# Reciprocal softmax sums for the values' product: float16 halves through DMA transposes instead of float32 transposes on TensorE

## The chip, the core and the metric

One core of a Trainium2 chip runs one launch. The metric is device time in microseconds (us) from start to end of that launch, less being better. The engines are PE (TensorE, matrix products), DVE (VectorE), ACT (ScalarE), POOL (GpSimd) and SP (SyncE, which here only issues DMAs); each takes its instructions in the order in which the program lists them and waits on semaphores for the others.

## What is computed

A transformer block on x of 16 batches, 512 tokens, 512 channels, in float32: one normalised input feeds a causal 16-head attention and a gated feed-forward layer, and both are added to x.

```python
xn = _layernorm(x, axis=-1)
x = x + _L0_attn_ref(xn, w_qkv, b_qkv, w_out, b_out) + _L0_ffn_ref(xn, gate_w, up_w, down_w, gate_s, up_s, down_s)
# attention: 16 heads of 32 channels
scores = jnp.einsum('bhqd,bhkd->bhqk', q, k) / math.sqrt(Hd) + causal[None, None]
attn = jax.nn.softmax(scores, axis=-1)
out = jnp.einsum('bhqk,bhkd->bhqd', attn, v)
# feed-forward: 1408 inner channels
hdn = jax.nn.silu(g) * u
```

The kernel does the softmax without dividing: it makes exp(score - row maximum), multiplies these by the values, and divides the product by the row sums. What the change is about is how the reciprocals of the row sums reach the place where that division is made. The sums lie one query per partition, as 16 columns (4 query blocks x 4 heads); the product of a group of four heads lies the other way, 4 heads x 32 channels on the partitions and 512 queries along the row. So each reciprocal has to be repeated over 32 channels and transposed.

## The kernel before, in words

Weights stay in SBUF. All float32 operands of products are split in two 16-bit halves, a high one and the rest, so that a product is three matmuls with 16-bit operands (two for the feed-forward layer, whose weights are small integers).

The program is not written in the order in which it runs. It is a list of steps, each with an engine, an assumed duration, the buffers that it reads and writes, and, for PE, a key: the time at which it should run. `Plan.order` (line 98) simulates the five engines with these durations, picks for PE the ready step of lowest key and for the others the one that is ready first (`slack` shifts that), and hands out the numbered buffers as it goes. The order it finds is the order of the instructions on every engine, fixed at build time. If the chip takes other times than the assumed ones, an engine waits at the instruction whose input is late, and everything listed behind it on that engine waits too.

The work is cut into 64 slots, one for each of 16 batches and 4 groups of four heads (loop at line 916). A slot holds

- the scores of its own group, in three pieces (`soft_run`, line 505): query block 3, block 2, blocks 1 and 0. Behind each piece come row maxima on DVE (L556), exponentials on ACT, which also sum the rows into `den` (L561), the split of the exponentials into two halves `pq` on ACT (L581) and DVE (L586), and a DMA transpose `pT<-pq` for each query block, issued by SP (L595);
- the values' product `av` of the group of the slot before (`av_step`, line 601), at 7 us (`AV_LAG`) into the slot by its key;
- fillers: the q and k projections of the next group (`qk_proj`), some of the 11 feed-forward chunks of the batch (`ffn_chunk`), the v projections of the batch in the first slot (`v_proj`), the output projection of the batch before in the second, the down projection in the fourth.

In `av_step` the reciprocals travel so: DVE takes them (`rden`, L615), POOL spreads each over 32 columns as float32 (`rb`, L618), PE transposes four 128x128 squares into a PSUM bank (`R`, L628), ACT copies that to SBUF (`Rs`, L631), DVE multiplies the product by it (L654), and ACT and POOL split the result in halves `oh` and `ol` (L655, L656) for the output projection.

Buffers that matter here: the tag `mm`, three PSUM banks, through which all projections, the feed-forward products and `R` go; the tag `tmp32`, four buffers of 512 float32, for the q, k projection (`qkt`), the v projection (`vt`), the feed-forward chunk (`ft`) and `rb`; the tag `r32`, one such buffer, for `Rs`; one PSUM bank for `av`.

Of the kernel before, what the change touches and what calls it, by code (L numbers as in the profile page):

```python
# [9 lines left out]
F16 = mybir.dt.float16  # L10
# [4 lines left out]
ALU = mybir.AluOpType  # L15
# [6 lines left out]
P = 128  # L22
# [3 lines left out]
NG = H // 4  # L26
# [3 lines left out]
def newton_rsqrt(nc, y, v, t):  # L30

    yi = y.bitcast(I32)
    nc.vector.tensor_scalar(yi, v.bitcast(I32), 1, None, ALU.logical_shift_right)
    nc.vector.tensor_scalar(yi, yi, -1, 0x5F3759DF, ALU.mult, ALU.add)
    for _ in range(3):
        nc.vector.scalar_tensor_tensor(t, v, -0.5, y, ALU.mult, ALU.mult)
        nc.vector.tensor_tensor(t, t, y, ALU.mult)
        nc.vector.scalar_tensor_tensor(y, t, 1.5, y, ALU.add, ALU.mult)


class Tile:
# [21 lines left out]
class Plan:  # L63
# [34 lines left out]
    def order(self):  # L98
        for n, st in enumerate(self.steps):
            st.n, st.left = n, len(st.deps)  # L100
            for d in st.deps:
                d.next.append(st)
        free = dict.fromkeys(self.ENGINES, 0.0)
        ready = {e: [] for e in self.ENGINES}
        made, done, dma = {}, [], 0.0

        def begin(st):
# [12 lines left out]
            return t  # L120

        def release(st):
            st.at = max([d.end - d.lat * (d.eng == st.eng != "SP") for d in st.deps], default=0.0)
            ready[st.eng].append(st)

        for st in self.steps:
            if not st.left:
                release(st)
        while len(done) < len(self.steps):
            best = None  # L130
            for e in self.ENGINES:
# [32 lines left out]
def fast_path(ctx, tc, good, x, wqkvT, bqk, bv, woT, bo, wgT, wuT, wdT, gs, us, dsc, out):  # L164
# [3 lines left out]
    nc = tc.nc  # L168
# [50 lines left out]
    wd = cp.tile([P, IC, D], F8, name="wd")  # L219

    st = [dict() for _ in range(NB)]
    grp = {}
    NSLOT = NB * NG
    MM4 = 0.864

# [14 lines left out]
                step.key = t  # L240
                t += dur * k

    def mm_group(f, ps, ops, piece=4, first=0, n=None):


        n = len(ops) if n is None else n

        def run(k0, k1):
            for k in range(k0, k1):
                l, r = ops[k][0]()  # L250
                nc.tensor.matmul(ps(), l, r, start=(first + k == 0), stop=(first + k == n - 1))  # L251

        prev = []
# [189 lines left out]
    def qk_proj(f, b, g, which):  # L443
        s = st[b]
        off = which * 512 + g * P
        nm = f"{b}_{g}_{which}"
        ps, t = mm("qk_" + nm), tmp32("qkt_" + nm)
# [17 lines left out]
            r=[ps, "bqk"], w=[t], slack=-3,  # L465
# [4 lines left out]
            r=[t, h], w=[l] + (["first"] if b == 0 and g == 0 else []), slack=-3,  # L470
# [3 lines left out]
    def v_proj(f, b, tb):  # L474
        s = st[b]
        ps, t = mm(f"v_{b}_{tb}"), tmp32(f"vt_{b}_{tb}")
        if tb == 0:
# [27 lines left out]
    def soft_run(b, g, blocks):  # L505
# [31 lines left out]
        def exps(i):  # L537
# [2 lines left out]
        both = lambda t: [(t, i) for i in blocks]  # L540
        run = add(
            "PE", 0.3 + 3 * cols / 2400.0, scores, r=[qh, ql, kh, kl],
            w=[tok for t in pss for tok in both(t)] + ([f"slot{b * NG + g}"] if blocks[0] == 3 else []),
            lat=0.3,
        )
        for u, i in enumerate(blocks):
# [27 lines left out]
        for i in blocks:  # L574
# [21 lines left out]
                r=[(pq, i, 0), (pq, i, 1)], w=[("pT", i)], lat=0.19 * 8 * (i + 1), slack=-5,  # L596
            )
            base += 8 * n
        return run

    def av_step(b, g):
# [6 lines left out]
        rb = work("rb_" + nm, "tmp32", 4)  # L608
# [7 lines left out]
        add(  # L616
            "POOL", gps(512),
            lambda: nc.gpsimd.tensor_scalar(  # L618
                rb().rearrange("p (c d) -> p c d", d=32),
                rden().unsqueeze(2).to_broadcast([P, 16, 32]),  # L620
                2.0 ** -15, None, ALU.mult,
            ),
            r=[rden], w=[rb],
        )

        def spread():
            for i in range(4):
                nc.tensor.transpose(R()[:, i * P : (i + 1) * P], rb()[:, i * P : (i + 1) * P], ident)  # L628

        first = add("PE", 0.5, spread, r=[rb], w=[R], lat=0.3)  # L630
        add("ACT", act(512), lambda: nc.scalar.copy(r(), R()), r=[R], w=[r], slack=-3)  # L631

        def run():
            for side, k0 in ((0, 0), (1, 0), (0, 1), (1, 1), (0, 2), (0, 3)):
# [12 lines left out]
                            skip_group_check=True,  # L647
                        )

        second = add(  # L650
            "PE", 2.3, run, r=[("pT", i) for i in range(4)] + [(t, tb) for t in (vh, vl) for tb in range(NT)],
            w=[av], lat=0.3,
        )
        add("DVE", dve(512), lambda: nc.vector.tensor_tensor(r(), av(), r(), ALU.mult), r=[av, r], w=[r], slack=-2)  # L654
        add("ACT", act(512), lambda: nc.scalar.copy(oh(), r()), r=[r], w=[oh], slack=3)  # L655
        add("POOL", gps(512), lambda: nc.gpsimd.tensor_tensor(ol(), r(), oh(), ALU.subtract), r=[r, oh], w=[ol])  # L656
        return first, second


    def ffn_chunk(f, b, ic):  # L660
# [129 lines left out]
        )  # L790

    def count_good(when, key):
        ps, ps1, limits = mm("flagT"), mm("flagR"), tmp32("limits")
# [40 lines left out]

    def attention_slot(s):

        av, runs = (), []
        if s > 0:
            av = av_step(*divmod(s - 1, NG))
        if s < NSLOT:  # L840
            b, g = divmod(s, NG)
            grp[(b, g)] = dict(den=work(f"den_{b}_{g}", "den", 2, (P, 16)))
            runs = [(soft_run(b, g, bl), sum((i + 1) * P + 250 for i in bl)) for bl in ((3,), (2,), (1, 0))]

        def place(t0, T):
            for k, step in enumerate(av):
                step.key = t0 + AV_LAG + (k - 1) * 1.5
# [301 lines left out]
```

## Time and profile before

| What | Value |
|---|---|
| time, median of 3 runs (lowest to highest) | 1915.01 us (1914.96 to 1915.26) |
| profiled execution, whole | 1915.52 us |
| its span, first to last instruction | 1913.7 us |
| mean granted clock of TensorE | 0.997 |
| SP's queue: 256 DMA transposes pT<-pq | 5.5 us from issue to landing, median |
| DMA packets of the hardware queue | 65.7% of 16 engines' span |
| chip memory traffic over the span | 38 GB/s |

How to read the page that the prediction quotes. A group line says: line, engine, operation, output<-inputs, shape, count, then busy time in us, mean ns of one, then the idle time of the engine just before such instructions and who ended it. The busy time of PE is the union of modelled durations of pipelined matmuls; what a matmul costs PE when it is kept fed is the distance from its start to the start of the next one, read from the timeline. A DMA row's time runs from issue to landing. A window row gives, for each engine, how many us of that window it was busy, and at its end the granted clock (1.00 is full) and the share of the 16 DMA engines in use.

### The profile page before, as it was taken

What the parts mean: (1) busy time and instruction counts of PE and PEld (TensorE: products, weight loads), DVE (VectorE), ACT (ScalarE), POOL (GpSimd) and SP (SyncE); (2) the same over time, 40 slices, a digit from 0 to 9 for tenths busy, and PEclk for the clock granted to TensorE, in tenths of its full rate; (3) what the DMA queues carried; (4) which work ended last, traced back from release to release, by engine and by line L of the source; (5) the groups of instructions that cost most, each with busy time, mean ns of one, the idle gap of its engine ahead of it and who ended that gap; (6) DMA issues with size and microseconds to landing.
All of it is one profiled execution on the core that took longest, in us unless ns stands there. A gap on an engine that the chain in (4) does not pass through costs nothing. (4 is left out here: it accounts for less than half of the span.)

```text
span 1913.7 us, 40913 instructions
## 1 busy us (share of the span) xinstructions
PE 1877.3 (98%) x15250; PEld 892.2 (47%) x15250; DVE 1482.0 (77%) x3541; ACT 1335.2 (70%) x3185; POOL 983.5 (51%) x713
## 2 busy tenths in 40 slices
PE   7899999999999999999999999999999999999997
PEld 3344444444444444444444444444444444444443
DVE  7778778797887978878788787877869787686674
ACT  5766757677676776767767676776767767677673
POOL 4446455464554646456464554645546454564533
PEclk9999999999999999999999999999999999999999
DMA  9875757666676656767567586667766667666465
GB/s 169 144 127 120 133 128 154 129 130 121 132 153 128 145 109 138 143 135 144 110 133 144 122 148 123 139 121 140 153 127 135 119 136 148 127 130 106 97 118 115
DMA packets 769519, 252.39 MB, mean 132 GB/s; under 512 B 734368, under 2 KB 738848, under 8 KB 769312
## 3 DMA queue, kind: packets, MB, share of 16 engines
q1 hardware_dynamic: 764688, 247.54, 65.7%
q0 software_dynamic: 4624, 2.16, 1.4%
q8 instruction: 121, 1.98, 0.4%
q14 instruction: 86, 0.70, 0.1%
HBM read 55.85 MB, written 16.78 MB: 38 GB/s over the span
## 5 line engine op out<-in xcount | busy, mean ns | idle before, releaser
L561 ACT ACTIVATE p<-s,negm 128x512 f32<-128x512 f32 (+3 forms) x1024 | 529.0, 531 | 231.3 <-DVE negm L556 229.1
L586 DVE SCALAR_TENSOR_TENSOR pq<-p,pq 128x2048 f16<-128x2048 f32 (+3 forms) x256 | 425.7, 1676 | 238.5 <-ACT pq L581 229.2
L556 DVE CUSTOM_DVE_ANT_0 s<-s,mask 128x512 f32<-128x512 f32 (+3 forms) x1024 | 473.1, 517 | 53.0 <-PE s L527 45.2
L581 ACT ACTIVATE pq<-p 128x2048 f16<-128x2048 f32 (+3 forms) x256 | 324.0, 1291 | 10.3 <-DMA pT<-pq 8.4
L691 POOL TENSOR_TENSOR hl<-ft,hh 128x512 f16<-128x512 f32 x176 | 226.9, 1295 | 190.1 <-ACT hh L690 189.3
L469 POOL TENSOR_TENSOR qkl<-qkt,qkh 128x512 f16<-128x512 f32 x128 | 165.1, 1290 | 244.7 <-ACT qkh L467 233.9
L251 PE MATMUL g<-xh,wg 128*128 128x512 f16 x704 | 267.6, 380 | 4.3 <-ACT qkt L464 2.4
L251 PE MATMUL u<-xh,wu 128*128 128x512 f16 x704 | 266.9, 379 | 2.8 <-DVE ft L681 1.5
L251 PE MATMUL dn<-wd,hh 128*128 128x512 fp8e4 x704 | 268.2, 381 | 0.0
L251 PE MATMUL dn<-wd,hl 128*128 128x512 fp8e4 x704 | 267.4, 380 | 0.0
L251 PE MATMUL g<-xl,wg 128*128 128x512 f16 x704 | 266.9, 379 | 0.0
L251 PE MATMUL u<-xl,wu 128*128 128x512 f16 x704 | 266.8, 379 | 0.0
L690 ACT CAST hh<-ft 128x512 f16<-128x512 f32 x176 | 109.3, 622 | 170.5 <-DVE ft L687 170.3
L618 POOL TENSOR_SCALAR rb<-rden 128x512 f32<-128x512 f32 x64 | 137.7, 2151 | 175.9 <-DVE rden L615 175.9
L251 PEld LDWEIGHTS <-wu 128*128 128x128 fp8e4 x1408 | 137.1, 98 | 169.7 <-issue 5.6
L561 ACT ACTIVATION_READ_ACCUMULATOR p<-s,negm 128x1 f32 x1024 | 214.5, 209 | 0.0
L251 PEld LDWEIGHTS <-wg 128*128 128x128 fp8e4 x1408 | 132.6, 98 | 159.6 <-issue 10.3
L251 PEld LDWEIGHTS <-wq_h 128*128 128x128 f16 x1024 | 95.4, 98 | 133.8 <-issue 28.5
L677 ACT ACTIVATE ft<-g,gt_c 128x512 f32<-128x512 f32 x176 | 121.1, 688 | 43.7 <-PE g L251 43.1
L407 POOL TENSOR_TENSOR xnl<-xc,xnh 128x512 f16<-128x512 f32 x60 | 96.7, 1612 | 104.5 <-DMA xl<-xnl 58.4
L687 DVE SCALAR_TENSOR_TENSOR ft<-u,gu_c,ft 128x512 f32<-128x512 f32 x176 | 132.0, 750 | 21.4 <-PE u L251 5.5
L717 POOL TENSOR_TENSOR xr<-xr,bo_b 128x512 f32<-128x512 f32 x64 | 94.4, 1475 | 103.9 <-DMA xr<-in_x 103.9
(114 smaller groups left out, 3205.3 us busy)
## 6 DMA issues: line engine op xcount, KB each, us to landing
xc<-in_x SPq DMA_DIRECT2D x64, 256.0 KB, 4.0
xr<-in_x SPq DMA_DIRECT2D x64, 256.0 KB, 2.9
out<-y SPq DMA_DIRECT2D x64, 256.0 KB, 2.5
pT<-pq SPq DMA_TRANSPOSE x256, 5.5
wq<-in_wqkvT SPq DMA_DIRECT2D x12, 256.0 KB, 5.4
exact<-in_wdT SPq DMA_DIRECT2D x11, 256.0 KB, 2.9
exact<-in_wgT SPq DMA_DIRECT2D x8, 256.0 KB, 3.0
exact<-in_wuT SPq DMA_DIRECT2D x8, 256.0 KB, 2.9
```

Source lines behind the costliest of these rows:

```text
L251: nc.tensor.matmul(ps(), l, r, start=(first + k == 0), stop=(first + k == n - 1))
L407: add("POOL", gps(512), lambda: nc.gpsimd.tensor_tensor(l(), xc(), h(), ALU.subtract), r=[xc, h], w=[l], slack=2)
L469: "POOL", gps(512), lambda: nc.gpsimd.tensor_tensor(l(), t(), h(), ALU.subtract),
L556: nc.vector.tensor_tensor_reduce(sc, sc, mask[:, 512 - n :], -(2.0 ** -7), 3e38, ALU.add, ALU.min, negm()[:, m : m + 1])
L561: nc.scalar.activation(exps(i).rearrange("p (k j) q -> p k j q", j=4)[:, :, j, :], part().rearrange("p (k q) -> p k q", q=P), AF.Exp, bias ...
L581: "ACT", act(4 * n), lambda src=src, half=half: nc.scalar.mul(half(0), src(), 2.0 ** 15),
L586: lambda src=src, half=half: nc.vector.scalar_tensor_tensor(half(1), src(), 2.0 ** 15, half(0), ALU.mult, ALU.subtract),
L618: lambda: nc.gpsimd.tensor_scalar(rb().rearrange("p (c d) -> p c d", d=32), rden().unsqueeze(2).to_broadcast([P, 16, 32]), 2.0 ** -15, Non ...
L677: "ACT", act(512) + 0.1, lambda: nc.scalar.activation(t(), pg(), AF.Tanh, scale=gt_c[:, ic : ic + 1]),
L687: lambda: nc.vector.scalar_tensor_tensor(t(), pu(), gu_c[:, ic : ic + 1], t(), ALU.mult, ALU.mult),
L690: add("ACT", act(512), lambda: nc.scalar.copy(hh(), t()), r=[t], w=[hh], slack=3)
L691: add("POOL", gps(512), lambda: nc.gpsimd.tensor_tensor(hl(), t(), hh(), ALU.subtract), r=[t, hh], w=[hl])
```

## The change

The reciprocals no longer go through PE. DVE takes `rden` as before and makes two float16 halves of it, scaled by 2^12; POOL spreads both halves over 32 columns (1024 float16 columns in place of 512 float32); SP issues a DMA transpose of that into an SBUF buffer `R`; POOL adds the two halves into the float32 factor `r`; DVE's multiplication takes the scale back. The four PE transposes and ACT's copy are gone.

```diff
-        R = mm("R_" + nm)
-        r = work("Rs_" + nm, "r32", 1)
+        rh = work("rh_" + nm, "rh", 2, (P, 2, 16), F16)
+        rb = work("rb_" + nm, "tmp32", 4, (P, 1024), F16)
+        R = work("R_" + nm, "r32", 1, (P, 8, P), F16)
+        r = tmp32("Rs_" + nm)
...
-        add("DVE", 0.15, lambda: nc.vector.reciprocal(rden(), d["den"]()), r=dens, w=[rden], slack=2)
+        def halves():
+            nc.vector.reciprocal(rden(), d["den"]())
+            nc.vector.tensor_scalar(rh()[:, 0, :], rden(), 2.0 ** 12, None, ALU.mult)
+            nc.vector.scalar_tensor_tensor(rh()[:, 1, :], rden(), 2.0 ** 12, rh()[:, 0, :], ALU.mult, ALU.subtract)
+
+        add("DVE", 0.6, halves, r=dens, w=[rden, rh], slack=2)
+        add(
+            "POOL", gps(1024),
+            lambda: nc.gpsimd.tensor_copy(
+                rb().rearrange("p (c d) -> p c d", d=32),
+                rh().rearrange("p z c -> p (z c)").unsqueeze(2).to_broadcast([P, 32, 32]),
+            ),
+            r=[rh], w=[rb],
+        )
+        add("SP", 1.3, lambda: nc.sync.dma_start_transpose(R(), rb()), r=[rb], w=[R], lat=1.5)
         add(
             "POOL", gps(512),
-            lambda: nc.gpsimd.tensor_scalar(
-                rb().rearrange("p (c d) -> p c d", d=32),
-                rden().unsqueeze(2).to_broadcast([P, 16, 32]),
-                2.0 ** -15, None, ALU.mult,
+            lambda: nc.gpsimd.tensor_tensor(
+                r(), R()[:, 0:4, :].rearrange("p i q -> p (i q)"), R()[:, 4:8, :].rearrange("p i q -> p (i q)"), ALU.add
             ),
-            r=[rden], w=[rb],
-        )
-
-        def spread():
-            for i in range(4):
-                nc.tensor.transpose(R()[:, i * P : (i + 1) * P], rb()[:, i * P : (i + 1) * P], ident)
-
-        first = add("PE", 0.5, spread, r=[rb], w=[R], lat=0.3)
-        add("ACT", act(512), lambda: nc.scalar.copy(r(), R()), r=[R], w=[r], slack=-3)
+            r=[R] + when, w=[r],
+        )
...
-        add("DVE", dve(512), lambda: nc.vector.tensor_tensor(r(), av(), r(), ALU.mult), r=[av, r], w=[r], slack=-2)
+        add("DVE", dve(512), lambda: nc.vector.scalar_tensor_tensor(r(), av(), 2.0 ** -27, r(), ALU.mult, ALU.mult), r=[av, r], w=[r], slack=-2)
```

`when` names the scores of blocks 1 and 0 of the same group, which the row sums come from anyway. The planner gets three further rules for the order on PE: no step may be picked whose key is over 20 us (`AHEAD`) beyond the lowest key still open; the q and k projections of a slot come after the last scores of the slot two before; the v projections of a batch come after the last values' product of the batch before.

```diff
+                if e == "PE":
+                    cands = [c for c in cands if c[1].key <= keys[-1][0] + AHEAD]
...
+            after=last_scores[b * NG + g - 2 : b * NG + g - 1] if b * NG + g > 1 else (),
...
+            after=[grp[(b - 1, NG - 1)]["step"]] if b else (),
```

The check values `limits`, used once near the end, move from a `tmp32` buffer to one of tag `xr`. Nothing else changes; all durations that the planner assumes for the other steps stay.

More of the change, by code (lines that the diff above doesn't have):

```diff
@@ L38, in newton_rsqrt @@
         nc.vector.scalar_tensor_tensor(y, t, 1.5, y, ALU.add, ALU.mult)
+AHEAD = 20.0
 class Tile:
@@ L105, in order @@
         made, done, dma = {}, [], 0.0
+        keys = sorted((s.key, s.n) for s in self.steps if s.eng == "PE")[::-1]
         def begin(st):
@@ L130, in order @@
             best = None
+            while keys and self.steps[keys[-1][1]].end is not None:
+                keys.pop()
             for e in self.ENGINES:
                 cands = [(max(t, free[e]), st) for t, st in ((begin(st), st) for st in ready[e]) if t is not None]
+                if e == "PE":
+                    cands = [c for c in cands if c[1].key <= keys[-1][0] + AHEAD]
                 if not cands:
@@ L221, in fast_path @@
     st = [dict() for _ in range(NB)]
-    grp = {}
+    grp, last_scores = {}, []
     NSLOT = NB * NG
@@ L241, in place, with mm_group @@
                 t += dur * k
-    def mm_group(f, ps, ops, piece=4, first=0, n=None):
+    def mm_group(f, ps, ops, piece=4, first=0, n=None, after=()):
         n = len(ops) if n is None else n
@@ L251, in run @@
                 nc.tensor.matmul(ps(), l, r, start=(first + k == 0), stop=(first + k == n - 1))
-        prev = []
+        prev = after
         for k0 in range(0, len(ops), piece):
@@ L542, in soft_run @@
             "PE", 0.3 + 3 * cols / 2400.0, scores, r=[qh, ql, kh, kl],
-            w=[tok for t in pss for tok in both(t)] + ([f"slot{b * NG + g}"] if blocks[0] == 3 else []),
+            w=[tok for t in pss for tok in both(t)] + {3: [f"slot{b * NG + g}"], 1: [f"slot{b * NG + g}c"]}.get(blocks[0], []),
             lat=0.3,
@@ L598, in soft_run, with av_step @@
             base += 8 * n
+        if blocks[0] == 1:
+            last_scores.append(run)
         return run
-    def av_step(b, g):
+    def av_step(b, g, when):
         d = grp[(b, g)]
@@ L607, in av_step @@
         rden = work("rden_" + nm, "rden", 2, (P, 16))
-        rb = work("rb_" + nm, "tmp32", 4)
-        R = mm("R_" + nm)
-        r = work("Rs_" + nm, "r32", 1)
+        rh = work("rh_" + nm, "rh", 2, (P, 2, 16), F16)
+        rb = work("rb_" + nm, "tmp32", 4, (P, 1024), F16)
+        R = work("R_" + nm, "r32", 1, (P, 8, P), F16)
+        r = tmp32("Rs_" + nm)
         oh = work("oh_" + nm, "oh", 5, dt=F16)
@@ L648, in run @@
                         )
-        second = add(
+        step = add(
             "PE", 2.3, run, r=[("pT", i) for i in range(4)] + [(t, tb) for t in (vh, vl) for tb in range(NT)],
@@ L653, in av_step @@
         )
-        add("DVE", dve(512), lambda: nc.vector.tensor_tensor(r(), av(), r(), ALU.mult), r=[av, r], w=[r], slack=-2)
+        add("DVE", dve(512), lambda: nc.vector.scalar_tensor_tensor(r(), av(), 2.0 ** -27, r(), ALU.mult, ALU.mult), r=[av, r], w=[r], slack=-2)
         add("ACT", act(512), lambda: nc.scalar.copy(oh(), r()), r=[r], w=[oh], slack=3)
         add("POOL", gps(512), lambda: nc.gpsimd.tensor_tensor(ol(), r(), oh(), ALU.subtract), r=[r, oh], w=[ol])
-        return first, second
+        d["step"] = step
+        return step
     def ffn_chunk(f, b, ic):
@@ L792, in count_good @@
     def count_good(when, key):
-        ps, ps1, limits = mm("flagT"), mm("flagR"), tmp32("limits")
+        ps, ps1, limits = mm("flagT"), mm("flagR"), work("limits", "xr", 1)
         m = cp.tile([48, 1], F32, name="flag_max")
@@ L835, in attention_slot @@
     def attention_slot(s):
-        av, runs = (), []
-        if s > 0:
-            av = av_step(*divmod(s - 1, NG))
+        av, runs = None, []
         if s < NSLOT:
@@ L842, in attention_slot @@
             grp[(b, g)] = dict(den=work(f"den_{b}_{g}", "den", 2, (P, 16)))
+        if s > 0:
+            av = av_step(*divmod(s - 1, NG), [f"slot{s - 1}c"])
+        if s < NSLOT:
             runs = [(soft_run(b, g, bl), sum((i + 1) * P + 250 for i in bl)) for bl in ((3,), (2,), (1, 0))]
         def place(t0, T):
-            for k, step in enumerate(av):
-                step.key = t0 + AV_LAG + (k - 1) * 1.5
+            if av:
+                av.key = t0 + AV_LAG
             t = t0
```

## The prediction

> **What bounds the kernel now.** I read the busy line of the page first, then the same by stretches of the span, to see whether one engine carries every stage.
>
> ```profile
> span 1913.7 us, 40913 instructions
> PE 1877.3 (98%) x15250; PEld 892.2 (47%) x15250; DVE 1482.0 (77%) x3541; ACT 1335.2 (70%) x3185; POOL 983.5 (51%) x713
> ...
> 200.00:600.00 400.00, 398.87 (x3270) 190.20 (x3271) 316.00 (x746) 284.28 (x674) 207.41 (x147) 1.00 0.67 131
> 600.00:1000.00 400.00, 400.00 (x3236) 189.73 (x3238) 319.06 (x772) 282.30 (x680) 218.30 (x151) 1.00 0.66 133
> 1000.00:1400.00 400.00, 399.68 (x3287) 190.39 (x3284) 317.98 (x757) 284.32 (x685) 210.96 (x146) 1.00 0.71 136
> 1400.00:1880.00 480.00, 479.88 (x3946) 228.80 (x3945) 359.47 (x865) 337.12 (x804) 241.41 (x184) 1.00 0.65 125
> ```
>
> PE (first number after the window's length) is idle for 1.6 us in 1680 at full clock, while DVE, ACT, POOL and the DMA engines (0.65 to 0.71) have room. A busy share of modelled durations could hide slack between matmuls, so the timeline of PE around one pass of the reciprocals comes next.
>
> ```profile
> 936.58 0.59 PE L251 MATMUL qk<-xh,wq_l 128*128 128x512 f16 x2
> 937.01 0.60 PE L628 MATMUL R<-ident,rb 128*128 128x128 f32 x4
> 937.45 0.38 PE L251 MATMUL dn<-wd,hh 128*128 128x512 fp8e4 x1
> 937.66 0.38 PE L251 MATMUL dn<-wd,hl 128*128 128x512 fp8e4 x1
> ```
>
> Start to start, a 512-column matmul takes 0.216 us and the next follows at once: PE is packed, and what is taken off it shortens the time unless a wait takes its place. The waits of PE from 60 to 1890 us say how few there are; all lie before 220 us except 0.3 us on `pT` and a last one of 0.1 on the same.
>
> ```profile
> PE R L628 <- POOL rb L618: 2.9, 1, 2.9
> PE g L251 <- ACT qkt L464: 2.4, 1, 2.4
> PE g L251 <- DVE y L739: 1.5, 1, 1.5
> ```
>
> **What is removed.** Four transposes per group: 937.01 to 937.45 is 0.44 us; over the trace each transposes' distance to the next start has the median 0.109, so 4 x 0.109 = 0.436, and 64 x 0.436 = 27.9 us off PE. (All 256 distances, stalls and changes of tile shape included, sum to 29.7.) Here a page of the Trainium skill gives another price: "TensorE: Matmul & The Clock Gate", Part 4 (PE-mode transpose), has some 275 ns for a transpose in a kernel. The trace's record of one is 273 ns, so the page is right about that; but by it the sum would be 256 x 0.275 = 70 us, by the row's distances 28. The record is the latency, more than half of it overlapped by neighbours. I take 27.9. ACT loses 64 copies of 0.61 us (39 us, off the path), and `R` no longer holds one of the three `mm` banks for the 1.3 to 3.3 us (2.4 median) from its transposes to the end of ACT's copy: worth nothing where PE never waits, so zero to 4 us, the waits of the first 220 us; I take zero. The single wait of 2.9 us on `rb` disappears, but that start-up stretch is reshuffled, so I bank none of it.
>
> **What is added, and what covers it.**
>
> DVE: two instructions on 128x16. Not in the trace; between the 0.16 us of such instructions on 128x4 and the 0.24 of the reciprocal. Taking 0.17, 64 x 0.34 = 22 us: DVE 77% to 78%. The multiplication becomes another form over the same 512 columns (0.68 for both kinds in the trace): nothing.
>
> POOL: the spread grows from 512 float32 to 1024 float16 columns, and an add of 512 comes in. Rows:
>
> ```profile
> L618 POOL TENSOR_SCALAR rb<-rden x64: 1482/2260/2547, 53.0 to 1890.3; 128x512 f32<-128x512 f32 x64
> ...
> L656 POOL TENSOR_TENSOR ol<-Rs,oh 128x512 f16<-128x512 f32 x64 | 96.7, 1511 | 86.8 <-ACT oh L655 86.8
> ...
> L586 DVE SCALAR_TENSOR_TENSOR pq<-p,pq 128x512 f16<-128x512 f32 x64 | 66.1, 1033 | 0.5 <-ACT pq L581 0.5
> ```
>
> The copy is between 1.5 us (if bytes count) and 4.5 (twice the median 2.26); I take 3.0, twice the undisturbed 1.48, since elements count on the nearest row. The add is 1.16 undisturbed, 1.5 on average. POOL gets 64 x (3.0 + 1.5 - 2.15) = 150 us, 51% to 59%: no bound.
>
> But the copy stands beside the `pq` splits of blocks 1 and 0, and there a rule speaks against the change: "SBUF — State Buffer", Who interferes with whom, says that a DVE instruction with two SBUF inputs and a GpSimd instruction that reads SBUF share a port, and that the first to start holds it for its whole length. The trace agrees in part: `rb` takes 2.3 us where it overlaps a `pq` and 1.49 where not, the `pq` of 512 columns 1.09 beside POOL against 0.69. By the rule in full, a 3.0 us copy could hold back `pq`, and so block 0's DMA, by 3.0 us in each slot. The product `av` starts a median 2.6 us after its last `pT` landed (about 1.1 in every fourth slot); taking 3.0 from every slot's own margin leaves PE 56 us of waits. By the row the present 1.48 us copy costs `pq` 0.4, twice as long a copy 0.7 to 1: 3 to 5 us of waits. I take 3 us, by the row, which is this kernel's own, with 56 as the far end.
>
> SP: one more transpose of 128x1024 per slot, the very shape of block 0's `pT`, whose 64 instances have a median 1.56 us to issue and 3.5 to land (3.0 to 6.1). SP's queue grows by 64 x 1.56 = 100 us, from 1079 us of issuing (56% of the span) to 62%. The 16 engines are busy 1035 us each with 256-byte packets for 5600 transposed squares; 512 more are 9%, or 5 points above the 66% now. In SP's order it meets blocks 1 and 0. Before them it would put 1.6 us ahead of the last `pT`; behind them it waits for one issue. The order is planned with 1.3 + 1.5 us for it, close to the rows, so `av` is re-placed accordingly; I charge nothing in the steady slots, and the far end is the 1.6 us off each margin, some 15 us.
>
> Who waits for it: POOL's add, with `hl` and `qkl` of the fillers queued behind; then DVE's multiplication, with the row maxima and `ft` behind. The new path from `rden` to a finished `r`: 0.57 (DVE) + 0.4 (to POOL's start, as now) + 3.0 + 1.6 (one SP issue) + 3.5 + 1.2 = 10.3 us. The old one had time until the multiplication: from 60 slots after the start, `rden` to multiplication is at least 9.5 us, then 11.7, median 13.6. So at 10.3 one slot is late by 0.8, and DVE's lateness reaches PE only after the banks are full, one 8-matmul fill of 1.7 us later. Zero; what it costs otherwise is the first rival.
>
> Buffers: `r` leaves its own `r32` buffer for `tmp32`, and `R` takes `r32`. One `tmp32` of four is then held through `av` until `ol` is made (the copy's end to `ol`'s end is a median 9.8 us now), while `rb` is freed earlier, when its DMA has landed, not when PE comes round (5.4 us after it was ready). Net some 5 us of one buffer in a 29 us slot. The planner's order sees this. The three ordering rules name what the buffers enforced; 20 us is two thirds of a slot, more than the 11 us by which `av` trails its slot's start in the timeline. Zero, bounded by -3 to +10.
>
> Tail: the last group has nothing to hide behind. Now `rden` is at 1890.0, the last `pT` lands 1897.8, `av` ends 1899.3, the multiplication starts 1899.5. The new DMA follows or precedes that `pT`: landing about 1.5 us after 1897.8, plus the add of 1.2, is 1900.5 to 1901. Cost 1.5 us.
>
> **Sum.** 1915.5 (profiled execution; its span is 1913.7) - 27.9 + 3 (port) + 1.5 (tail) = 1892.1. The median of the runs lies 0.5 below the profiled one: 1891.6.
>
> **Rivals.**
>
> 1. Slower: DVE waits for `r`. Its place is the multiplication, in DVE's order ahead of the bank readers. If the copy takes 4.5, POOL is busy when R lands (2.7 for a disturbed add's predecessor, 2.3 for the add), and SP and landing take 1.9 and 4.4, `r` comes after about 16 us in place of 10.3. Against the margins of the 60 slots, less 1.7 us that the banks cover, 16 us costs PE 52 us: 1915 - 27.9 + 1.5 + 52 = 1941. It decides from about 15.2 us, where the loss eats the gain. For it: all four delays are seen singly in the trace; against it: they would have to meet in most slots, and the planner places the multiplication by when `r` is ready. Chance 0.13.
>
> 2. No change: the margin of `pT` goes. The port's hold and the new transpose together take about 2 us from each slot's margin: 25 us of waits on `pT`, 1915 - 27.9 + 1.5 + 25 = 1914. For it: the slots with 1.1 us. Against: part of the loss is planned for. Chance 0.07.
>
> 3. The same mechanism as forecast with part lost, 5 to 15 us more of waits: 1896 to 1906. Chance 0.15, and it counts as faster.
>
> 4. More gained than forecast, because bank pressure and the early waits go as well: 1915 - 29.7 - 3 = 1882. Chance 0.10. That nothing shows at all because PE isn't the bound is excluded by the windows above.
>
> My forecast, 1891.6, within 1884 to 1896, has 0.55. The range reaches from 1883 to 1912: it leaves out rival 1, most of rival 2 and a little of rival 4. A change under 0.2% (4 us) can't be told from none with this kernel.
>
> **What would show it.** Right: no L628 rows; the windows from 200 to 1880 still with PE idle below 1%; four slots taking 1.7 us less; SP's transposes landing at 3.5 to 4.5 us; POOL near 59%. Rival 1: a group "DVE Rs waits for POOL" of tens of us, with PE waiting for `ft`. Rival 2: PE `av` waiting for DMA `pT<-pq`. The port: `pq` of 512 columns well above 1.03 us. Wrong altogether: early or mid-kernel PE waits on `qkt` or `y` of several us per slot, which would say that the new order of PE itself, with fewer banks and buffers in reach, costs more than the transposes did.

## The result, and the profile after

| | before | after |
|---|---|---|
| time, median (lowest to highest), 6 runs each | 1914.54 us (1912.92 to 1915.26) | 1945.97 us (1942.9 to 1947.78) |
| ratio after to before | | 1.0162 [1.015, 1.0173] |
| profiled execution; its span | 1915.5; 1913.7 us | 1943.1; 1941.1 us |
| mean granted clock of TensorE | 0.997 | 0.988 |
| PE's listed waits, whole span | 27.8 us | 59.8 us |

The kernel became 1.6% slower. 1891.6 us was forecast, within 1883 to 1912, and slower had a chance of 0.13. The page's busy line and the windows of the changed kernel, in the order in which those of before were read:

```profile
span 1941.1 us, 40593 instructions
PE 1874.7 (97%) x14994; PEld 866.5 (45%) x14994; DVE 1571.6 (81%) x3669; ACT 1323.6 (68%) x3121; POOL 995.7 (51%) x777
...
200.00:600.00 400.00, 391.77 (x3181) 181.54 (x3180) 329.71 (x762) 277.31 (x651) 209.50 (x159) 0.99 0.71 136
600.00:1000.00 400.00, 390.84 (x3117) 180.39 (x3116) 330.14 (x780) 271.92 (x646) 207.43 (x159) 0.99 0.71 141
1000.00:1400.00 400.00, 392.67 (x3123) 180.79 (x3121) 325.72 (x765) 280.58 (x661) 204.06 (x158) 0.99 0.73 143
1400.00:1880.00 480.00, 472.29 (x3850) 219.57 (x3848) 388.39 (x896) 332.65 (x786) 248.22 (x199) 0.99 0.69 133
```

The 256 transposes are gone from PE's count (15250 less 14994). But PE, idle for 1.6 us of these 1680 before, is now idle for 32.4 (8.2, 9.2, 7.3 and 7.7), and the granted clock is 0.99 in every window. POOL, which was forecast to grow most, stays at 51%; DVE is at 81%. PE's waits name one place:

```profile
PE v L260 <- DVE ft L703: 31.4, 13, 2.9
PE lnT L432 <- DVE xc L402: 10.6, 1, 10.6
PE s L538 <- ACT p L572: 6.7, 9, 1.4
PE u L260 <- DVE ft L703: 3.7, 3, 2.0
PE op L260 <- ACT oh L676: 2.3, 1, 2.3
PE av L662 <- DMA pT<-pq: 2.2, 2, 2.0
```

The columns are the total in us, the number of times and the longest. Before, PE never waited in the v projection; now it does so 13 times, once in nearly every batch, for DVE's first reading of a feed-forward bank (`ft`, L703). The other lines together weigh what they did before (28.4 us against 27.8), and `pT`, which the forecast watched, holds PE for 2.2 us.

**The place.** The timeline of PE around one such wait (start, length, what was waited for in brackets):

```profile
1110.54 1.03 PE L260 MATMUL v<-wq_h,xl 128*128 128x512 f16 x4
1114.48 1.42 PE L260 MATMUL v<-wq_h,xh 128*128 128x512 f16 x4 [2.92 <-DVE ft L703]
```

PE stands still for 2.92 us because all three `mm` banks are full, and the first to be emptied waits for L703. DVE, at that time, is busy with something else: the layer norm of the next batch, 13 instructions on 128x4 that make the reciprocal root by three Newton steps (L391, L392 and L33 to L38), all but L392 in a row in which each needs the one before. DVE first, then POOL over the same stretch:

```profile
1108.57 0.17 DVE L391 TENSOR_SCALAR ln_v<-mv 128x4 f32<-128x4 f32 x1
...
1109.58 0.16 DVE L38 SCALAR_TENSOR_TENSOR ln_y<-ln_t,ln_y 128x4 f32<-128x4 f32 x1
1109.77 1.10 DVE L36 SCALAR_TENSOR_TENSOR ln_t<-ln_v,ln_y 128x4 f32<-128x4 f32 x1
1110.91 1.19 DVE L37 TENSOR_TENSOR ln_t<-ln_t,ln_y 128x4 f32<-128x4 f32 x1
1112.13 0.16 DVE L38 SCALAR_TENSOR_TENSOR ln_y<-ln_t,ln_y 128x4 f32<-128x4 f32 x1
1112.33 1.11 DVE L36 SCALAR_TENSOR_TENSOR ln_t<-ln_v,ln_y 128x4 f32<-128x4 f32 x1
...
1113.75 0.68 DVE L703 SCALAR_TENSOR_TENSOR ft<-ft,g 128x512 f32<-128x512 f32 x1
```

```profile
1109.70 1.16 POOL L713 TENSOR_TENSOR hl<-ft,hh 128x512 f16<-128x512 f32 x1 [4.02 <-ACT hh L712]
1110.82 1.26 POOL L739 TENSOR_TENSOR xr<-xr,bo_b 128x512 f32<-128x512 f32 x1
1112.16 1.26 POOL L740 TENSOR_TENSOR y<-y,xr 128x512 f32<-128x512 f32 x1
```

Three DVE instructions that take 0.16 us elsewhere take 1.10, 1.19 and 1.11. Each starts as, or after, a POOL instruction starts (1109.70, 1110.82, 1112.16) and ends when that one ends (1110.86, 1112.08, 1113.42). From its first instruction to L703 the chain takes 5.2 us. The same place before, DVE and then POOL:

```profile
1094.15 0.17 DVE L382 TENSOR_SCALAR ln_v<-mv 128x4 f32<-128x4 f32 x1
...
1096.33 0.16 DVE L38 SCALAR_TENSOR_TENSOR ln_y<-ln_t,ln_y 128x4 f32<-128x4 f32 x1
1096.41 0.68 DVE L681 SCALAR_TENSOR_TENSOR ft<-ft,g 128x512 f32<-128x512 f32 x1
```

```profile
1096.37 1.16 POOL L691 TENSOR_TENSOR hl<-ft,hh 128x512 f16<-128x512 f32 x1 [3.83 <-ACT hh L690]
1097.48 1.27 POOL L717 TENSOR_TENSOR xr<-xr,bo_b 128x512 f32<-128x512 f32 x1
```

The chain ran in 2.3 us, and its last instruction started 0.04 us before `hl` did. Neither chain, nor `hl`, nor `xr` is touched by the diff. What moved is the distance between them. From the chain's start to `hl` it was 2.22 us and is 1.13: in the order that the planner now finds, one of the four row statistics ahead of the chain (L384) has gone from before the row maxima to behind the pair of `ft` instructions, so that the chain begins later against `hl`. The planner's own distance went from 2.2 to 1.4 us, with the chain assumed at 2.0 and no interference in its model.

**The second charge.** Behind most of these waits the clock is halved. The windows before, in and behind one such stretch (the last three columns are the clock, the DMA share and GB/s):

```profile
1107.00:1115.00 8.00, 5.08 (x45) 2.34 (x44) 7.44 (x19) 2.59 (x4) 3.64 (x3) 1.00 0.01 2
1115.00:1118.40 3.40, 3.40 (x10) 1.22 (x9) 3.40 (x8) 1.42 (x3) 2.06 (x2) 0.50 0.05 10
1118.40:1121.00 2.60, 2.60 (x14) 1.17 (x13) 2.48 (x14) 2.60 (x15) 1.04 (x1) 1.00 1.16 216
```

10 matmuls in 3.4 us, against 14 in the next 2.6. A stretch of 3.41 us at half clock lost 1.7 us of work. There were 2 such stretches before (at 115 us and at the end) and 14 after, 10 of them behind a wait in v.

Which wait is followed by one is not chance alone. The starts of all 14 stretches lie whole multiples of 3.413 us apart (the first two behind a wait in v start at 401.59 and 521.06 us, 119.47 or 35 times 3.413 apart). If time is cut at these multiples, the ten batches that lost the clock had 2.10 us or more of their wait inside one cell, and the three that kept it (waits of 2.14, 2.14 and 2.27 us) 1.98 us or less, as the cut fell inside the wait. This is read from the trace of the changed kernel; no run was made to test it.

**The sum, as measured.** I count a batch from the start of its v projection to the next one's. Before: 116.54 us. Less the 4 x 0.436 of the transposes that is 114.80. After: 117.4 to 117.5 in the batches with a wait of 2.1 to 2.3 us and full clock, 119.0 to 119.8 where the half clock follows. Over the span: 1913.7 - 27.9 + 31.4 (v waits) + 0.6 (other waits) + 17.5 (clock: 0.009 of 1941) = 1935.3. Of the remaining 5.8 us to 1941.1, 3.4 belong to the transposes: where nothing waits, a batch takes 115.01 us and not 114.80 (experiment 1). The other 2.4 I can't itemise; the rounding of the clock to 0.001 alone is worth 1.9.

### The profile page after: what moved, and what is told of

It is laid out like the page before. It is cut to its first block, busy times and chain, and to the rows that moved or that the text cites. A ratio compares the mean times of both kernels' runs of the same rounds, so it can differ in the third digit from the quotient of the medians.

```text
span 1941.1 us, 40593 instructions
## 1 busy us (share of the span) xinstructions
PE 1874.7 (97%) x14994; PEld 866.5 (45%) x14994; DVE 1571.6 (81%) x3669; ACT 1323.6 (68%) x3121; POOL 995.7 (51%) x777
## 3 DMA queue, kind: packets, MB, share of 16 engines
q1 hardware_dynamic: 832272, 264.33, 69.7%
## 5 line engine op out<-in xcount | busy, mean ns | idle before, releaser
L597 DVE SCALAR_TENSOR_TENSOR pq<-p,pq 128x2048 f16<-128x2048 f32 (+3 forms) x256 | 454.4, 1789 | 182.3 <-ACT pq L592 182.3
L713 POOL TENSOR_TENSOR hl<-ft,hh 128x512 f16<-128x512 f32 x176 | 232.8, 1323 | 281.2 <-ACT hh L712 281.1
L592 ACT ACTIVATE pq<-p 128x2048 f16<-128x2048 f32 (+3 forms) x256 | 320.0, 1280 | 8.8 <-DMA pT<-pq 6.8
L479 POOL TENSOR_TENSOR qkl<-qkt,qkh 128x512 f16<-128x512 f32 x128 | 177.3, 1385 | 176.2 <-ACT qkh L477 174.1
L703 DVE SCALAR_TENSOR_TENSOR ft<-ft,g 128x512 f32<-128x512 f32 x176 | 119.6, 680 | 72.2 <-ACT ft L699 71.4
L639 POOL COPY rb<-rh 128x1024 f16<-128x1024 f16 x64 | 77.7, 1215 | 149.4 <-DVE rh L633 149.4
L677 POOL TENSOR_TENSOR ol<-Rs,oh 128x512 f16<-128x512 f32 x64 | 91.6, 1432 | 99.2 <-ACT oh L676 99.2
```

Of the source, the lines that this page charges most:

```text
L479: "POOL", gps(512), lambda: nc.gpsimd.tensor_tensor(l(), t(), h(), ALU.subtract),
L592: "ACT", act(4 * n), lambda src=src, half=half: nc.scalar.mul(half(0), src(), 2.0 ** 15),
L597: lambda src=src, half=half: nc.vector.scalar_tensor_tensor(half(1), src(), 2.0 ** 15, half(0), ALU.mult, ALU.subtract),
L703: "DVE", dve(512), lambda: nc.vector.scalar_tensor_tensor(t(), t(), 1.0, pg(), ALU.add, ALU.mult),
L713: add("POOL", gps(512), lambda: nc.gpsimd.tensor_tensor(hl(), t(), hh(), ALU.subtract), r=[t, hh], w=[hl])
```

## The experiments

My theory, called A: the Newton chain now lies beside POOL's `hl`, `xr` and `y`, its two-input instructions are held by them one after another, L703 comes late, PE stops in v and the clock drops. Two rivals: the parts that were added are the cause (POOL's copy and add, the longer DVE work, the wait for `r`; in the expectations B where DVE waits for `r`, D where the load itself slows things); or the new order on PE is, whatever DVE and POOL do beside each other. What each expects of a run is said in words with it.

Two things about the comparisons. The kernel before was timed again beside each group of experiments, with medians from 1913.03 to 1914.41 us, so a difference between two experiments is good to a few us. And the order of the instructions, as the traces have it: experiments 1, 2 and 7 keep that of the changed kernel, but for the instructions that are left out or replaced, and experiment 6 that of the kernel before, but for the added pair. Experiments 3 and 4 are planned anew. Experiments 5 and 8 differ from their kernel in the first 245 us on PE and DVE and keep its order there from then on.

**1. One Newton step in place of three** (in the changed kernel; the last two refinements are left out). This shortens the victim and leaves the order.

```diff
-    for _ in range(3):
+    for _ in range(1):
```

> The changed kernel with one Newton step in place of three in the reciprocal square root of the layer norm (two steps, six of its small DVE instructions, are left out, so the norm is less exact); every engine keeps the order of all other instructions. Theory A (the stall is DVE's chain of small layer-norm instructions, 5.3 us in the changed kernel against 2.3 before, placed ahead of the DVE instruction that empties a feed-forward PSUM bank, for which PE's v projection waits): the chain falls to 1.5 to 3 us, PE's wait of 2.1 to 2.9 us per batch and the half clock after it go, time 1888 to 1900. Rival B (DVE waits for late reciprocals), and rival D (the added POOL, SP and DMA work slows everything): unchanged, 1940 to 1948.

Measured: 1891.73 us (1888.67 to 1893.69), ratio to before 0.9892 [0.9875, 0.9908]. No wait in v, clock 0.996, the chain at 1.17 us. From 600 to 1000 us PE is never idle:

```profile
600.00:1000.00 400.00, 400.00 (x3267) 186.16 (x3266) 335.74 (x790) 285.63 (x677) 217.37 (x166) 1.00 0.74 146
```

Taking out six DVE instructions of 0.16 us per batch (15 us of DVE's time over the whole launch, which isn't the bound) gives 54 us. A few tenths of arithmetic can't do that; a collision that goes away can. All that the change added (copy, DMA, add) is still there, and PE's order is the same, so the added parts or PE's order as the main cause are out.

**2. The same number of instructions, with one SBUF input each** (changed kernel; the refinement's arithmetic is replaced by scalings).

```diff
-        nc.vector.scalar_tensor_tensor(t, v, -0.5, y, ALU.mult, ALU.mult)
-        nc.vector.tensor_tensor(t, t, y, ALU.mult)
-        nc.vector.scalar_tensor_tensor(y, t, 1.5, y, ALU.add, ALU.mult)
+        nc.vector.tensor_scalar(t, v, -0.5, None, ALU.mult)
+        nc.vector.tensor_scalar(t, t, 2.0, None, ALU.mult)
+        nc.vector.tensor_scalar(y, y, 1.0, None, ALU.mult)
```

> The changed kernel with the same number of Newton instructions on the same sizes, but each with one SBUF input instead of two (the three refinements are left out, the norm keeps its first guess); order of all engines the same. If the chain is long because its two-input instructions wait for the POOL instruction that runs beside them (A with the port): the chain takes 2.3 to 2.6 us as in the kernel before, PE's wait per batch goes, 1888 to 1900. If it is long for its number of instructions or for another reason: chain over 4.5 us, time 1938 to 1948. Rivals B and D: unchanged time, whatever the chain does.

Measured: 1903.65 us (1903.11 to 1907.19), ratio 0.9957 [0.994, 0.9973]. The chain takes 3.60 us where it lies beside POOL and 1.74 alone; the waits in v are 13 as before, but of 0.5 to 1.2 us, and no half clock follows.

```profile
PE v L260 <- DVE ft L703: 9.6, 13, 1.2
```

A miss: a chain of 2.3 to 2.6 us and 1888 to 1900 us were expected. DVE, then POOL at the place say why:

```profile
1088.30 1.13 DVE L38 TENSOR_SCALAR ln_y<-ln_y 128x4 f32<-128x4 f32 x1
1089.34 0.16 DVE L36 TENSOR_SCALAR ln_t<-ln_v 128x4 f32<-128x4 f32 x1
1089.53 1.12 DVE L37 TENSOR_SCALAR ln_t<-ln_t 128x4 f32<-128x4 f32 x1
```

```profile
1088.25 1.15 POOL L713 TENSOR_TENSOR hl<-ft,hh 128x512 f16<-128x512 f32 x1 [3.99 <-ACT hh L712]
1089.36 1.26 POOL L739 TENSOR_TENSOR xr<-xr,bo_b 128x512 f32<-128x512 f32 x1
```

The two instructions that start just behind the start of `hl` or of `xr` are held to its end, as those with two inputs were; the one between, which starts as `hl` ends and just ahead of `xr`, is not. The chain is shorter by itself (1.74 us in place of 2.35), so it meets two POOL instructions and not three. So the edit didn't take the hold away. The run speaks for the collision, but it can't show that two inputs are its condition. The trace of the changed kernel says the same: a `TENSOR_SCALAR` from SBUF to SBUF that starts under a running POOL instruction of about 1 us or more takes longer (`xc`, L402: 1.38 us against 0.54; `rh`, L632: 0.48 against 0.17; medians of 4 and 5 cases), while the row statistics (L384) and `ft<-ft,g` (L703), which reads one input from PSUM, keep their 0.68 us there.

**3. Only the high halves** (changed kernel; the low halves of the reciprocals are left out, and with them half the copy, half the DMA and POOL's add; DVE multiplies by `R` directly).

```diff
-            "POOL", gps(1024),
+            "POOL", gps(512),
...
-        add(
-            "POOL", gps(512),
-            lambda: nc.gpsimd.tensor_tensor(
-                r(), R()[:, 0:4, :].rearrange("p i q -> p (i q)"), R()[:, 4:8, :].rearrange("p i q -> p (i q)"), ALU.add
-            ),
-            r=[R] + when, w=[r],
-        )
```

> The changed kernel with the high halves of the reciprocals alone (the low halves are left out): POOL's spread has 512 columns, the DMA transpose half the squares, POOL's add is gone and DVE multiplies by the float16 factor itself. If what delays is POOL's add, held up behind a DVE split, and DVE waiting for it (B, or A with B as its start): the chain meets fewer POOL instructions, PE's wait falls below 1 us per batch, 1888 to 1905. If only the chain's place in DVE's order counts (A alone): the wait stays, 1930 to 1946. If the DMA and POOL load counts (D): half of the loss comes back, 1915 to 1930.

Measured: 1916.42 us (1915.08 to 1918.94), ratio 1.0018 [1.0009, 1.0027]. The time lies in the range that was given to the added load (D), the waits are those that A expected:

```profile
PE v L260 <- DVE ft L695: 24.6, 14, 2.0
```

The chain still takes 5.3 us beside `hl`, `xr` and `y`. Without most of the added parts that the rival blames, the waits are nearly all there: 1.8 to 2.0 us in each of 13 batches, which without the transposes gives the batch 116.99 us, about as long as before (116.54). What is missing is the half clock, not once in those 13: no wait puts more than 1.83 us into one cell of the 3.413 us grid. So A missed the time because a wait that is shorter by some tenths lost its second charge. The missing half clock (10 times 1.7 us) and the shorter waits (31.4 less 24.6 us) account for 24 of the 30 us between this kernel and the changed one.

**4. The chain in four pieces for the planner** (changed kernel; same instructions, but other steps may come between them).

```diff
-        add("DVE", 2.0, rstd, r=[(mv, tb) for tb in range(NT)], w=[v, y, t], slack=slack)
+        add("DVE", 0.6, rstd, r=[(mv, tb) for tb in range(NT)], w=[v, y, t], slack=slack)
+        for _ in range(3):
+            add("DVE", 0.6, lambda: newton_step(nc, y(), v(), t()), r=[v, y, t], w=[y, t], slack=slack)
```

> The changed kernel with its whole computation; the layer norm's chain is given to the planner as four steps instead of one, so that other DVE work can be placed between them; in the new order the feed-forward bank is emptied after the first piece and a split, ahead of the three Newton steps. A: the wait per batch falls to below 1 us and the clock stays up, 1888 to 1905, faster than both kernels. B and D: 1938 to 1948.

Measured: 1918.8 us (1913.24 to 1921.95), ratio 1.0025 [1.0016, 1.0033]. The waits in v are gone (0.3 us), but from 200 to 1880 us the new order has a wait of its own, for the exponentials:

```profile
PE s L547 <- ACT p L581: 9.1, 32, 0.4
```

A miss: 1888 to 1905 was expected. 27 us better than the change, and none better than before; all waits of PE in that stretch (11.8 us) explain about 12 of the 27 us that are missing against 1891.7, the rest I have not settled. A new plan brings its own accidents, so a repair should leave the order alone.

**5. POOL held back** (changed kernel, the whole computation). One tiny POOL copy that reads the chain's result is put ahead of the two POOL instructions that collide with it, so they start when the chain is done.

```diff
+            y = st[b + 1]["ln"][1]
+            hold = add("POOL", 0.15, lambda y=y: nc.gpsimd.tensor_copy(scratch, y()), r=[y], w=["scratch"])
+            st[b][("hl", 1)].deps.add(hold)
+            if b > 0:
+                st[b - 1][("xr", NT - 1)].deps.add(hold)
```

> The changed kernel with its whole computation and one more POOL instruction per batch, a copy of the 128x4 result of the layer norm's chain to a scratch tile, placed before the three POOL instructions (hl, xr, y) that ran beside the chain; it makes them start only after the chain's end. The order on PE, DVE and ACT stays. If the chain is long only because these three hold the port (theory A): chain 2.3 to 2.4 us, PE's wait per batch 0 to 0.6 us, no half clock behind it, 1888 to 1897, faster than both kernels. If the chain's place in the order alone costs: PE's wait stays above 1.5 us, 1925 to 1946. If POOL's later start costs as much elsewhere: PE waits on other things, 1905 to 1940.

Measured: 1892.01 us (1891.77 to 1893.87), ratio 0.9893 [0.9876, 0.9909]. One window, and POOL at the place:

```profile
600.00:1000.00 400.00, 399.53 (x3261) 185.86 (x3260) 337.90 (x811) 283.01 (x671) 218.82 (x169) 1.00 0.74 145
```

```profile
1083.00 0.19 POOL L955 COPY scratch<-ln_y 128x4 f32<-128x4 f32 x1 [5.27 <-DVE ln_y L38]
1083.14 1.16 POOL L714 TENSOR_TENSOR hl<-ft,hh 128x512 f16<-128x512 f32 x1
```

`hl` starts behind the chain, which is back at 2.35 us; no wait in v, no half clock. An added instruction and an added wait make the kernel 54 us faster. Some 3.5 us of this come from the first batch, where the order on PE changed too (126.37 us in place of 129.84); nearly all the rest comes in batches in which PE and DVE have the changed kernel's order. This is the fastest kernel here with the whole computation, and it beats both.

**6. The collision brought into the kernel before** (before, same order; one more statistics pair inside the chain, 0.85 us, moves its end under `hl`).

```diff
+            if b > 0:
+                nc.vector.bn_stats(bs()[:, NT - 1, :], s["xs"][NT - 1]())
+                nc.vector.bn_aggr(mv()[:, NT - 1, :], bs()[:, NT - 1, :])
             newton_rsqrt(nc, y(), v(), t())
```

> The kernel before, transposes on TensorE and all, with one repeated pair of statistics instructions (0.8 to 0.9 us, the same values again) ahead of the Newton steps in each batch, in the same planned order. Theory A says that the kernel before escapes the collision by less than 0.1 us (its last Newton instruction starts at +2.18 us of the chain, POOL's hl at +2.22), so that a shift of 0.85 us brings it about without any of the change: chain over 4.5 us, PE waits of 1 to 3 us per batch on the feed-forward bank, half clock behind some, 1940 to 1975. If the stall belongs to the new path of the reciprocals (B, D): only the extra DVE time, hidden or once per batch, 1914 to 1928.

Measured: 1930.78 us (1929.38 to 1932.35), ratio 1.009 [1.0073, 1.0107]. DVE, then POOL:

```profile
1106.97 1.07 DVE L38 SCALAR_TENSOR_TENSOR ln_y<-ln_t,ln_y 128x4 f32<-128x4 f32 x1
1108.07 1.19 DVE L36 SCALAR_TENSOR_TENSOR ln_t<-ln_v,ln_y 128x4 f32<-128x4 f32 x1
...
1109.57 0.68 DVE L684 SCALAR_TENSOR_TENSOR ft<-ft,g 128x512 f32<-128x512 f32 x1
```

```profile
1106.86 1.16 POOL L694 TENSOR_TENSOR hl<-ft,hh 128x512 f16<-128x512 f32 x1 [3.84 <-ACT hh L693]
1107.98 1.27 POOL L720 TENSOR_TENSOR xr<-xr,bo_b 128x512 f32<-128x512 f32 x1
```

```profile
PE v L251 <- DVE ft L684: 8.7, 13, 0.7
```

The same stretched instructions and the same wait of PE in 13 batches, in a kernel that has nothing of the change. 0.85 us of DVE work became 2.7 us of delay and 17 us of time. The time is over the 1914 to 1928 of the rivals and under the 1940 to 1975 of A: the wait is smaller than I expected (0.7 us), the clock stays at 0.997, and the batch is longer (117.8 against 116.54) by more than the wait that is listed.

**7. The chain moved forward by less statistics** (changed kernel; two of the four row statistics read only their first 64 columns).

```diff
-                nc.vector.bn_stats(bs()[:, tb, :], xc())
+                nc.vector.bn_stats(bs()[:, tb, :], xc()[:, :64] if b and tb > 1 else xc())
```

> The changed kernel with the last two of the four layer-norm statistics of each batch taken over the first 64 columns instead of 512 (so that part of the statistics is left out); the order on all engines stays. It takes some 0.9 us of DVE time per batch away, directly ahead of the chain, so that the chain starts about 0.9 us earlier against POOL's hl, the mirror of the run that delayed it in the kernel before. Theory A (a matter of where the chain lies against POOL's three instructions): the chain meets at most its last instruction or two, 2.4 to 3.6 us, PE's wait per batch falls from 2.1-2.9 us to 0-0.5 us, 1888 to 1899. If DVE is only short of time there: the wait falls by no more than the 0.9 us given back, to 1.2 us or more, 1908 to 1933.

Measured: 1897.62 us (1895.61 to 1902.0), ratio 0.9921 [0.9905, 0.9938]. The chain begins earlier against `hl`, takes 3.24 us, and no wait in v is left. It is moved, not shortened: 0.9 us less work ahead of it is worth 48 us. If DVE had only been short of time there, PE's wait of 2.1 to 2.9 us would have fallen by 0.9 us at most.

**8. The hold of experiment 5 in the kernel before.** Is its gain a gain in any case?

> The kernel before with the same extra POOL instruction as in m_guard, which holds the three POOL instructions back until the layer norm's chain has ended. Theory A: the kernel before has next to no collision that it could take away, so no change, 1910 to 1918. If the instruction does good by itself (by delaying POOL's work, whatever the reciprocals do): faster by over 8 us, below 1906.

Measured: 1909.52 us (1906.55 to 1911.39), ratio 0.9976 [0.9967, 0.9984]. That is just under the 1910 to 1918 of A. The steady batches stay as they were (116.54 us, some up to 117.05); the gain is in batch 1, where the kernel before had a collision too (chain 4.21 us, batch 120.51, now 116.54). So in steady batches the hold repairs what the new order broke, and it is not a gain of its own. With the hold in both, the change of the reciprocals itself is worth 1909.5 to 1892.0: 17.5 us, or 15.9 by the two ratios to the kernel before.

## Why the prediction was wrong

**The step that failed** is the port, the term "I take 3 us, by the row", together with "zero, bounded by -3 to +10" for the order. What they put at 3 us and at nothing came to 31.4 us of waits in v, and to some 17 us of half clock behind them, for which the forecast had no term. I weighed the rule of the Trainium skill ("SBUF — State Buffer", Who interferes with whom: the first to start of a two-input DVE instruction and a reading POOL instruction holds the shared port for its whole length) against one victim only, `pq`, and one margin, that of `pT`. There the sum by the row came close: `pq` of 512 columns went from 1.03 to 1.25 us, and PE waits 2.2 us for `pT` in place of 1.2. The far end of 56 us, by the rule in full, was looked for in the wrong place. The rule held for instructions that the diff doesn't touch: 128x4 instructions of the layer norm with two SBUF inputs, each held to the end of the POOL instruction that it met. Its price can be read from two rows, before and then after:

```profile
L36 DVE SCALAR_TENSOR_TENSOR ln_t<-ln_v,ln_y 128x4 f32<-128x4 f32 x48 | 7.8, 162 | 1.7
```

```profile
L36 DVE SCALAR_TENSOR_TENSOR ln_t<-ln_v,ln_y 128x4 f32<-128x4 f32 x48 | 33.2, 691 | 1.6
```

25 us of DVE's time in one line; with the like in L37 (0.16 to 0.44 us on average), the chain grows by 2.9 us, and of these 2.1 to 2.9 reach PE in 13 batches, since three banks cover only the rest.

What made the collision is the order. I said that the planner "sees this", and bounded what its new order could cost by the buffers' margins. But the planner knows no interference, and the place had a margin of 0.04 us that stood in no list of waits, since before nothing waited there. Only a look at which POOL instruction starts next to the layer-norm chain would have shown it. My last sentence on what would be "wrong altogether" named PE's new order, with waits on `qkt` or `y`; it was DVE's and POOL's order, with a wait on `ft`.

**The three rules for PE's order** were taken as nothing. With them added to the kernel before, the planned order is the same step for step; leaving out `AHEAD` or the q and k rule leaves the changed kernel's plan as it is. Leaving out the v rule too changes PE's planned order up to 265 us only; from there on the plan has the same 1.4 us between the chain and `hl`. Those plans were compared as plans, not run.

**The steps that held.** The transposes: where nothing waits, in every steady batch of experiment 1 and in 5 of 13 of the hold kernel (experiment 5), a batch takes 115.01 us against 116.54, a gain of 1.53, where 1.74 were forecast; what the other 0.2 is I don't know. DVE: the two small halves take 0.20 and 0.22 us, estimated 0.17 each; that DVE is at 81% and not 78 comes from the instructions held by the port (L36, L37, and `pq` of 512 and 1024 columns, the latter 1.26 to 1.59 us). SP: `R` lands in 3.2 us (median; at most 5.5), 3.5 forecast, and DMA is at 69.7% of the engines, from 65.7. Tail: from the last `rden` to the end 25.2 us in the hold kernel, 23.7 before; 1.5 was forecast. And the sum: 1891.6 was forecast for this mechanism, 1892.0 is what the kernel takes with the collision removed. That agreement is partly luck: the hold also repaired batch 1, worth 4 us, and came with a first batch that is 3.5 us shorter, while the steady batches gained 1.2 us on average (116.62 to 115.44) in place of 1.74.

**Sizes that were off.** POOL's two new instructions:

```profile
L639 POOL COPY rb<-rh 128x1024 f16<-128x1024 f16 x64 | 77.7, 1215 | 149.4 <-DVE rh L633 149.4
L648 POOL TENSOR_TENSOR Rs<-R 128x512 f32<-128x512 f16 x64 | 82.2, 1285 | 21.5 <-DMA R<-rb 21.4
```

The copy of 1024 float16 took 1.2 us (1.04 undisturbed), less than the 1.5 of my low end: the float32 row with its multiplication was the wrong neighbour. So POOL is at 51%, not 59. Two small readings of the working were off as well: the 0.4 us to POOL's start is counted from the start of `rden`, so that the path is some 0.2 us shorter, and `R` held its bank for up to 6.2 us, over 3.3 in 4 of 64 cases. Nothing hangs on either.

**Rival 1** (DVE waits for `r`, 1941 us) has nearly the measured time, for another reason. Its path came close to the forecast (10.3): from `rden` to `r` 11.9 us median, up to 16.0. But the planner put the multiplication further back (15.8 us after `rden` in place of 13.8, medians), and DVE waited three times:

```profile
DVE Rs L675 <- POOL Rs L648: 9.6, 3, 7.5
```

A time that fits is no evidence for a mechanism; its own row decides, and rules it out here. Rival 2 had its row too, and that says 2.2 us.

**What stays open.** What exactly makes a DVE instruction liable to be held (experiment 2 was no test of it); whether the 3.413 us grid decides on the clock, as it seems to; what else the four-piece chain lost; the 0.2 us per batch that the transposes' gain falls short of, and 2.4 us in the sum of after. Taking away `hl`, `xr` and `y` themselves was not tried.

## What to carry to other kernels

Where an order is fixed at build time, a local saving is also a new order, so before forecasting look for the tight neighbours that it can shift: chains of small dependent DVE instructions, and which POOL instruction starts beside them, with the margin between the two in the timeline. A rule about interference has to be tried on every pair of such instructions that may become neighbours, not only on those that the change edits. When a saving doesn't arrive, look for the wait that is new by its place, and test it by holding back the disturber with the rest of the order left as it is.

## What the runs showed of the hardware

A DVE instruction of 0.16 us on 128x4 takes 1.1 to 1.2 us when it starts under a POOL instruction of that length, and a chain of them meets the next POOL instruction again: 2.35 us became 5.26. Instructions with two SBUF inputs were held so, and `TENSOR_SCALAR` with one; row statistics, and a two-input instruction that reads one input from PSUM, were not (0.68 us both ways).

PE's standing still for 2.14 to 2.92 us was followed by 3.41 us at half clock in 10 of 13 batches of the changed kernel; gaps of up to 2.02 us (13 batches of experiment 3) never were. In the changed kernel the length is not what divides them, but how much of the wait falls into one cell of a grid of 3.413 us on which all half-clock stretches start: 2.10 us or more lost the clock, 1.98 us or less kept it. This is no rule for all stages: in the first 130 us of other runs, cells with 1.8 us of standing still lost it too. So a wait just over 2 us cost up to 1.7 us more than its length.
